# Toeplitz matrices copied on GpSimd into channel-major order, one block of 24 channels ahead

## The chip, the cores and the metric

The kernel runs on one core of one Trainium2 chip. The metric is the device time of one execution in microseconds (us), the median over several runs; less is better. The engines are named as in the profile: PE is TensorE (PEld its weight loads), DVE is VectorE, ACT is ScalarE, POOL is GpSimd and SP is SyncE, which here only issues DMAs.

## The reference

Four residual layers act on an image batch of 8 x 56 x 56 x 192 in fp32: a gated Toeplitz mixer, shifted-window attention, a depthwise 3x3 convolution, and a selective scan in four directions. The change lies in the first. Cut to it:

```python
p = silu(x @ p_w.T + p_b); q = silu(x @ q_w.T + q_b); v = silu(x @ v_w.T + v_b)   # 576 channels
a1 = rpe_mlp(positions, t1...) * decay      # 112 x 576: one coefficient for each offset and channel
a2 = rpe_mlp(positions, t2...) * decay
qv = q * v
o1 = toeplitz(qv along w, a1)               # for each channel: a 56 x 56 Toeplitz matrix times qv
o2 = toeplitz(qv along h, a2)
x = x + (p * (o1 + o2)) @ o_w.T + o_b
```

So for each of 576 channels and each of two axes, a 56 x 56 matrix whose entry depends only on the difference of its indices multiplies all lines of the images along that axis.

## The kernel before

A short first part computes the coefficients of both axes and stores them in HBM as `ext[axis]`, 24 pieces of 112 offsets x 24 channels. The main part, the scan of all images, runs from about 3350 us to the end and is scheduled by hand. Between them stand `products` (it computes q times v for an image and stores it in HBM as `qv_d`) and `toeplitz` (it multiplies by the Toeplitz matrices and stores `o_d`). Both run first for images 0 to 3 alone. Then both run for images 4 to 7 beside the other layers of image 0: a loop takes a step of that front work and then, by an estimate of its cost, steps of `products` and `toeplitz`. Outside the main part the framework plans the order of the instructions on each queue; each queue then runs in order.

`toeplitz` loops over the two axes, in each over six slabs of 96 channels (`c0`), in each slab over four blocks of 24 channels (`c1`), in each block over six groups of four channels (`c2`).

- **Slab.** `x` (tile `tzx`, 112 x 112 x 96, 43 KB per partition) is loaded at line 261 by eight DMAs on SP, 588 KB each. A partition holds one position along the axis; two halves of the lines of an image lie in partitions 0 to 55 and 56 to 111. On the first axis a packet is 10752 bytes, on the second 384. There are three such buffers in the first use and two in the second. The results overwrite the slab in place, and eight DMAs on POOL store it at line 288.
- **Block.** `tm` (112 x 112 x 24) holds 24 Toeplitz matrices, each a block-diagonal pair of the same 56 x 56 matrix. It is made by the DMA itself: two DMAs on SP (line 270), one for each diagonal block, whose source lets row `p` start one offset later than row `p - 1`, so that every partition reads 56 x 24 consecutive numbers. The channel is therefore the innermost dimension. There are three such tiles, used in turn, cleared once by POOL memsets at line 249; the zero corners are never written again.
- **Group.** Each of four channels is one fp32 matmul at line 274, which the trace shows as two records. Its weights are `t[:, :, c2 + c]`, 112 numbers per partition with 96 bytes from one to the next. Its moving operand is `x[:, :, channel]`, 112 numbers with 384 bytes from one to the next. The four results share a PSUM bank, and one copy at line 280 (DVE and ACT in turn, DVE alone in the second use) brings them back into the slab.

`ps_tz` has eight PSUM banks in the first use and four in the second. Lines written 79 in the profile are the front work of image 0, recorded under a helper's line.

Of the kernel before, what the change touches and what calls it, by code (L numbers as in the profile page):

```python
# [15 lines left out]
F32 = mybir.dt.float32  # L16
# [9 lines left out]
CP = 96  # L26
D1 = 576
CH = 448
NCH = L // CH
TT = 112  # L30
# [4 lines left out]
TC = 24  # L35
# [49 lines left out]
def model(ctx: ExitStack, tc: tile.TileContext, a: dict, out: bass.AP):  # L85
    nc = tc.nc
# [16 lines left out]
    ext = [dram.tile([D1 // TC, TT, TC], F32, name=f"ext{i}") for i in range(2)]  # L103
# [45 lines left out]
    with tc.tile_pool(name="rpe", bufs=2) as rp, tc.tile_pool(name="rpe_ps", bufs=2, space=PSUM) as rps:  # L149
# [19 lines left out]
        for i in range(2):  # L169
# [19 lines left out]
            for c in range(6):  # L189
# [4 lines left out]
                out=ext[i].rearrange("n p c -> p n c"), in_=eT.rearrange("p k (n c) -> p (k n) c", c=TC)  # L194
# [44 lines left out]
    def toeplitz(images, beside):  # L239
        G = len(images) * (H // 2)  # L240
        with (
            tc.tile_pool(name="tz", bufs=2) as sp,
            tc.tile_pool(name="tz_t", bufs=1) as tp,
            tc.tile_pool(name="tz_ps", bufs=4 if beside else 8, space=PSUM) as ps,
        ):

            tm = [tp.tile([TT, TT, TC], F32, name=f"tm{i}") for i in range(3)]
            for t in tm:
                nc.gpsimd.memset(t, 0.0)
            n_t = 0  # L250
            for ax in range(2):
                along_h = "(h u w) c -> u h w c"
                along_w = "(u h w) c -> u w h c"
                stored = "(w u h) c -> u w h c"
                size = dict(h=H, u=2) if ax == 0 else dict(w=W, u=2)
                for c0 in range(D1 // CP):
                    x = sp.tile([TT, G, CP], F32, name="tzx", bufs=2 if beside else 3)
                    for n, b in enumerate(images):
                        v = qv_d[b][c0].rearrange(along_w if ax else along_h, **size)
                        for u in range(2):  # L260
                            nc.sync.dma_start(out=x[u * W : (u + 1) * W, n * 28 : (n + 1) * 28, :], in_=v[u])
                    for c1 in range(0, CP, TC):
                        t = tm[n_t % 3]
                        n_t += 1
                        e = ext[1 - ax][(c0 * CP + c1) // TC]

                        src = bass.AP(e.tensor, e.offset, [[TC, W], [1, W * TC]])
                        for u in range(2):
                            dst = t[u * W : (u + 1) * W, u * W : (u + 1) * W, :].rearrange("p i c -> p (i c)")
                            nc.sync.dma_start(out=dst, in_=src)  # L270
                        for c2 in range(0, TC, 4):
                            po = ps.tile([TT, 4, G], F32, name="ps_tz")
                            for c in range(4):
                                nc.tensor.matmul(  # L274
                                    po[:, c, :], t[:, :, c2 + c], x[:, :, c1 + c2 + c], start=True, stop=True
                                )
                            cs = slice(c1 + c2, c1 + c2 + 4)
                            copy = nc.vector.tensor_copy if (c2 // 4) % 2 or beside else nc.scalar.copy

                            copy(  # L280
                                x[:, :, cs].rearrange("p (b g) c -> p b g c", g=28)[:, :, ::-1, :],
                                po.rearrange("p c (b g) -> p b g c", g=28),
                            )
                            yield 1.0
                    for n, b in enumerate(images):
                        v = o_d[ax][b][c0].rearrange(stored if ax else along_h, **size)
                        for u in range(2):
                            nc.gpsimd.dma_start(out=v[1 - u], in_=x[u * W : (u + 1) * W, n * 28 : (n + 1) * 28, :])  # L288
# [3 lines left out]
    for stage in (products, toeplitz):  # L292
        for _ in stage(now, False):
            pass


    with (
# [51 lines left out]
        for i in range(WS):  # L349
            for u in range(2):  # L350
                for j in range(WS):
                    at = (i * 2 + u) * WS + j
                    nc.scalar.dma_start(
                        out=bias[at : at + 1, :, :, u, :],
                        in_=a["table"][:, WS - 1 - i : 2 * WS - 1 - i, WS - 1 - j : 2 * WS - 1 - j].unsqueeze(0),
# [792 lines left out]
        with tc.tile_pool(name="ps0", bufs=4 if later else 8, space=PSUM) as ps:  # L1148
            log = costs.setdefault("front", [])
            first, others, spent = front(0), (us for stage in (products, toeplitz) for us in stage(later, True)), 0.0  # L1150
            while log_of(first, log) is not None:
                spent += 0.55 * sum(cost for _, cost in log[-1])
                while later and spent > 0.0:
                    us = next(others, None)
                    if us is None:
                        break
                    spent -= us
            for _ in others if later else ():
                pass
        wp2 = own.enter_context(tc.tile_pool(name="w2", bufs=1))  # L1160
        sp = own.enter_context(tc.tile_pool(name="sc", bufs=2))
# [208 lines left out]
```

## Time and profile before

| what | value |
|---|---|
| median of 3 runs | 21839.35 us (21826.98 to 21850.64) |
| the profiled execution | 21800.17 us, of it 21798.4 us span |
| busy over the span | PE 84%, PEld 45%, DVE 73%, ACT 56%, POOL 69% |
| mean granted TensorE clock | 0.888 |
| first `toeplitz`, first axis | matmuls from 534.2 us; second axis ends at 1098.7 us |
| second `toeplitz` | matmuls from 2261 to 3346 us, beside the front work of image 0 |
| matmul records of line 274 | 4608, mean 403 ns each, overlapped; 1031.5 us busy together |
| weight loads of line 274 | 4608, mean 319 ns each, overlapped; 1028.0 us busy together |
| POOL while `toeplitz` runs | 192 DMA issues of 513 ns and 6 memsets of 2342 ns |

A group's row in the profile has its line, engine and operation, the tiles written and read, the shapes and the count; then the time that at least one of them was running, the mean time of one, and the idle time of the engine just before them with what ended it. Where records overlap, as matmuls and weight loads do, busy time divided by count is the pitch from one to the next, and the mean is longer than that. The stretches view gives, for chosen intervals of the span, the busy time and count of each engine, the granted clock, the busy share of the DMA engines and the bytes moved in a second.

### The profile page before, as it was taken

How to read it: one execution, taken by the hardware profiler on the slowest of the kernel's cores; microseconds unless marked ns; L12 is line 12 of the kernel's file. 1: busy time of each engine (PE TensorE's matmuls, PEld its weight loads, DVE VectorE, ACT ScalarE, POOL GpSimd, SP SyncE). 2: the span in 40 equal slices, each digit the busy share in tenths (PEclk: the TensorE clock that was granted, in tenths of full speed). 3: DMA queues.
4: the chain of work that ended last, by engine and by line, in shares of the span. 5: the costliest groups of instructions: out<-in, count | busy, mean ns of one | idle time of the engine just before them, and what ended most of it. 6: DMA issues, size and time to landing. Idle time of an engine off the chain costs nothing. (4 is left out here: it accounts for less than half of the span.)

```text
span 21798.4 us, 194536 instructions
## 1 busy us (share of the span) xinstructions
PE 18274.4 (84%) x58396; PEld 9706.4 (45%) x58396; DVE 15858.5 (73%) x12604; ACT 12098.2 (56%) x28153; POOL 15084.9 (69%) x9175
## 2 busy tenths in 40 slices
PE   7978977888888989888888889888988888887777
PEld 4845654444443434444444434443444444343333
DVE  2122117996799768986799769976898589976998
ACT  3126114655666466755666566746675566656555
POOL 0000006887789778977788768976898678877998
PEclk9588868999999989998999989998999899998888
DMA  3931575444544455445644455345544464445443
GB/s 86 245 98 49 170 196 169 126 135 159 187 143 135 136 184 170 129 129 171 184 133 136 154 184 150 123 150 170 169 129 140 156 185 132 135 155 175 134 138 116
DMA packets 2419572, 3249.82 MB, mean 149 GB/s; under 512 B 917598, under 2 KB 2361024, under 8 KB 2387554
## 3 DMA queue, kind: packets, MB, share of 16 engines
q1 hardware_dynamic: 2398292, 3121.12, 47.5%
q0 software_dynamic: 15520, 116.14, 1.4%
q8 instruction: 463, 7.59, 0.1%
q14 instruction: 593, 4.86, 0.1%
q10 hardware_dynamic: 4704, 0.12, 0.0%
HBM read 2661.35 MB, written 575.48 MB: 148 GB/s over the span
## 5 line engine op out<-in xcount | busy, mean ns | idle before, releaser
L1007 POOL TENSOR_TENSOR ring<-du,bm 128x896 f32<-128x896 f32 x5376 | 9447.8, 1771 | 1983.9 <-ACT ring L1014 1937.8
L1054 PE MATMUL ps_y<-hc,ident_sb 128*128 128x448 f32 x21504 | 9818.6, 591 | 590.2 <-POOL hc L1039 573.3
L1024 ACT ACTIVATE ps_a<-delta,A_logs_sb 128x449 f32<-128x449 f32 x10752 | 6858.4, 638 | 331.5 <-DVE ring L1033 68.7
L1054 PEld LDWEIGHTS ps_y<-hc,ident_sb 128*128 128x128 f32 x21504 | 4271.5, 207 | 4640.8 <-issue 3494.9
L1033 DVE TENSOR_TENSOR_SCAN ps_a<-ps_a,ring 128x898 f32<-128x898 f32 x2688 | 5429.0, 2020 | 1062.5 <-ACT ring L1014 555.0
L1033 DVE TENSOR_TENSOR_SCAN ring<-ps_a,ring 128x898 f32<-128x898 f32 x2688 | 5423.0, 2017 | 420.4 <-ACT state L1046 177.3
L1039 POOL TENSOR_TENSOR hc<-ring,cm 128x896 f32<-128x896 f32 x2688 | 4758.0, 1770 | 860.9 <-DVE ring L1033 349.3
L1039 DVE TENSOR_TENSOR hc<-ps_a,cm 128x896 f32<-128x896 f32 x2688 | 2935.0, 1092 | 974.5 <-PE ps_y L1054 753.3
L1046 ACT COPY state<-ps_a 128x2 f32<-128x2 f32 x2687 | 425.3, 158 | 3254.0 <-DVE hc L1039 3250.0
L280 DVE COPY tzx<-ps_tz 112x448 f32<-112x448 f32 x432 | 269.8, 625 | 1389.9 <-PE ps_tz L274 1175.0
L274 PE MATMUL ps_tz<-tzx,tm 112*112 112x112 f32 x4608 | 1031.5, 403 | 257.6 <-DMA tm<-ext 233.0
L288 POOL DMA_DIRECT2D o<-tzx x192 | 97.3, 513 | 1653.6 <-DVE tzx L280 1318.7
L274 PEld LDWEIGHTS ps_tz<-tzx,tm 112*112 112x112 f32 x4608 | 1028.0, 319 | 295.2 <-issue 288.7
L817 PE MATMUL ps_f<-slab 128*128 128x448 f32 x2646 | 1086.4, 546 | 69.9 <-DMA slab<-dg_d 62.1
L1046 ACT COPY state<-ring 128x2 f32<-128x2 f32 x2688 | 504.9, 188 | 791.3 <-DVE ring L1033 778.4
L647 PE MATMUL ps_f<-ident_sb,slab 98*98 98x98 f32 x1344 | 336.5, 326 | 619.6 <-ACT slab L640 619.6
L749 PE MATMUL ps_f<-slab 96*96 96x448 f32 x1764 | 725.1, 547 | 47.7 <-DVE slab L736 47.7
L817 PEld LDWEIGHTS ps_f<-slab 128*128 128x128 f32 x2646 | 506.8, 192 | 560.5 <-issue 485.0
L79 PE MATMUL ps_f<-slab 96*96 96x448 f32 (+6 forms) x2306 | 731.2, 497 | 10.2 <-DMA slab<-x 4.9
L990 POOL TENSOR_TENSOR du<-delta,xcd 128x448 f32<-128x448 f32 x672 | 658.6, 980 | 23.6 <-DMA xcd<-xc 23.6
L647 PEld LDWEIGHTS ps_f<-ident_sb,slab 98*98 98x98 f32 x1344 | 203.9, 158 | 1033.7 <-ACT slab L640 814.6
L227 PE MATMUL ps_qv<-wqv,xn 96*128 96x384 f32 (+1 forms) x1200 | 527.0, 522 | 128.2 <-DVE xn L146 67.5
(218 smaller groups left out, 17070.7 us busy)
## 6 DMA issues: line engine op xcount, KB each, us to landing
bm<-bc SPq DMA_DIRECT2D x1792, 448.0 KB
cm<-bc SPq DMA_DIRECT2D x1792, 448.0 KB
xcd<-xc SPq DMA_DIRECT2D x840, 224.0 KB
dl<-slab SPq DMA_DIRECT2D x224, 672.0 KB
delta<-dl SPq DMA_DIRECT2D x224, 672.0 KB
tzx<-qv SPq DMA_DIRECT2D x192, 588.0 KB
o<-tzx POOLq DMA_DIRECT2D x192, 588.0 KB, 13.7
slab<-x SPq DMA_DIRECT2D x224, 336.0 KB
```

Of the source, the lines that this page charges most:

```text
L79: return f(*args, **kw)
L274: nc.tensor.matmul(po[:, c, :], t[:, :, c2 + c], x[:, :, c1 + c2 + c], start=True, stop=True)
L647: nc.tensor.transpose(p[:PT_, e * PT_ : (e + 1) * PT_], S[:, 3 * g + e, :], ident[:PT_, :PT_])
L749: nc.tensor.matmul(p[:CP, :CH], dg[:, k, t, :], xp[:, u, k, dy : dy + 8, dx : dx + W], start=t == 0, stop=t == 8,)
L817: nc.tensor.matmul(p[:, :CH], dg[:, t, :], xp[:, 8 * j + dy : 8 * j + dy + 8, dx : dx + W], start=t == 0, stop=t == 8,)
L990: nc.gpsimd.tensor_mul(du[:, 0, :], deltas[i][:, d, 1 : CH + 1], xcs.pop((i, d)))
L1007: nc.gpsimd.tensor_mul(hs[:, :, tokens(i)[0]], dus[i, d].to_broadcast([128, NG, CH]), bms[i, k])
L1024: nc.scalar.activation(dA[:, n, :], deltas[i][:, d, at : at + CH + 1], AF.Exp, scale=negA[:, slot, d, c : c + 1])
L1033: nc.vector.tensor_tensor_scan(h, dA, hs, 0.0, ALU.mult, ALU.add)
L1039: (nc.gpsimd if on_pool(d, k) else nc.vector).tensor_mul(hc, h[:, :, tokens(i)[0]], cms[i, k])
L1046: nc.scalar.copy(states[i][:, d, NG * k : NG * k + NG], h[:, :, tokens(i)[2]])
L1054: nc.tensor.matmul(yps[i, d][:, :CH], ident, hcs[g][:, n, :], start=k + n == 0, stop=k + n == NP + NG - 2)
```

## The change

The three tiles that the DMAs fill are now called `rows`. A function `fetch(n)` issues the two DMAs of block `n` into one of them, takes a new tile `tms[n]` of 112 x 24 x 112 (two buffers in turn, 10.5 KB per partition each), and has POOL copy the block into it with the channel outermost: the copy reads the row in order and writes with 448 bytes from one element to the next. `fetch(0)` is called before the first slab; the loop over blocks calls `fetch` for the next block, over the ends of slabs and of the axis, before it takes its own. The matmul reads `t[:, c2 + c, :]`, 112 consecutive numbers per partition. Its moving operand, the evictions, the loads and stores of the slabs and the bytes moved stay as they are.

```diff
-            tm = [tp.tile([TT, TT, TC], F32, name=f"tm{i}") for i in range(3)]
-            for t in tm:
+            rows = [tp.tile([TT, TT, TC], F32, name=f"tr{i}") for i in range(3)]
+            for t in rows:
                 nc.gpsimd.memset(t, 0.0)
+            axes = (0, 1)
+            order = [(ax, n) for ax in axes for n in range(D1 // TC)]
+            tms = {}
+
+            def fetch(n):
+                if n >= len(order):
+                    return
+                ax, m = order[n]
+                e = ext[1 - ax][m]
+                tr = rows[n % 3]
+                src = bass.AP(e.tensor, e.offset, [[TC, W], [1, W * TC]])
+                for u in range(2):
+                    dst = tr[u * W : (u + 1) * W, u * W : (u + 1) * W, :].rearrange("p i c -> p (i c)")
+                    nc.sync.dma_start(out=dst, in_=src)
+                tms[n] = sp.tile([TT, TC, TT], F32, name="tm")
+                nc.gpsimd.tensor_copy(tms[n].rearrange("p c i -> p i c"), tr)
+
+            fetch(0)
             n_t = 0
-            for ax in range(2):
+            for ax in axes:
...
                     for c1 in range(0, CP, TC):
-                        t = tm[n_t % 3]
+                        fetch(n_t + 1)
+                        t = tms.pop(n_t)
                         n_t += 1
-                        e = ext[1 - ax][(c0 * CP + c1) // TC]
-                        src = bass.AP(e.tensor, e.offset, [[TC, W], [1, W * TC]])
-                        for u in range(2):
-                            dst = t[u * W : (u + 1) * W, u * W : (u + 1) * W, :].rearrange("p i c -> p (i c)")
-                            nc.sync.dma_start(out=dst, in_=src)
                         for c2 in range(0, TC, 4):
                             po = ps.tile([TT, 4, G], F32, name="ps_tz")
                             for c in range(4):
                                 nc.tensor.matmul(
-                                    po[:, c, :], t[:, :, c2 + c], x[:, :, c1 + c2 + c], start=True, stop=True
+                                    po[:, c, :], t[:, c2 + c, :], x[:, :, c1 + c2 + c], start=True, stop=True
                                 )
```

## The prediction

> **What bounds the kernel now.** I begin with the page's part 1, for the balance of the whole run.
>
> ```profile
> PE 18274.4 (84%) x58396; PEld 9706.4 (45%) x58396; DVE 15858.5 (73%) x12604; ACT 12098.2 (56%) x28153; POOL 15084.9 (69%) x9175
> ```
>
> An average of this kind covers stages with different limits, and the chain of waits is no help (every share in it is 0%). The edited function runs only before 3346 us, so I cut that part with the stretches view, for the `tm` tile alone, at the four uses of the function: four images along either axis alone (534 to 757, 757 to 1099 us), then four images beside other work (2261 to 2837, 2837 to 3346 us).
>
> ```profile
> core 0: us, PE busy (x) PEld busy (x) POOL busy (x), PEclk, DMA share, GB/s
> 534.00:757.00 223.00, 212.50 (x960) 211.56 (x960) 0.00 (x0) 0.50 0.81 253
> 757.00:1099.00 342.00, 297.92 (x1344) 296.27 (x1344) 0.00 (x0) 0.50 0.92 228
> 2261.00:2837.00 576.00, 262.70 (x1152) 264.17 (x1152) 0.00 (x0) 0.82 0.59 178
> 2837.00:3346.00 509.00, 258.12 (x1152) 255.79 (x1152) 0.00 (x0) 0.57 0.69 185
> ```
>
> Stage 1 is TensorE's: 212.5 of 223 us. In stage 2 a slab of 96 channels takes 50 us by the starts of its matmuls, only 42.6 of it on PE: the transfers set it. In stage 3 all PE work fills 500 of 576 us (same view without the tile). In stage 4 PE waits. Each fp32 matmul is two records (2304 calls, 4608 records). 212.50/960 is 221 ns a record, although stage 3 has nearly full clock and its 262.70/1152 is still 228 ns. So the clock does not set it; an operand does. The groups:
>
> ```profile
> L274 PE MATMUL ps_tz<-tzx,tm 112*112 112x112 f32 x4608 | 1031.5, 403 | 257.6 <-DMA tm<-ext 233.0
> L274 PEld LDWEIGHTS ps_tz<-tzx,tm 112*112 112x112 f32 x4608 | 1028.0, 319 | 295.2 <-issue 288.7
> L249 POOL MEMSET tm<- 112x2688 f32 x6 | 13.8, 2342 | 673.7 <-DMA qv<-qv 673.7
> L288 POOL DMA_DIRECT2D o<-tzx x192 | 97.3, 513 | 1653.6 <-DVE tzx L280 1318.7
> ```
>
> PEld is as full as PE (1028.0 against 1031.5): weight loads go end to end, 319 ns each, overlapped. The control is the transpose of 112x112 by the identity, with contiguous operands, in the lines of 1400 to 1500 us:
>
> ```profile
> L79 PE MATMUL ps_f<-ident_sb,slab 112*96 112x112 f32 x255 | 25.4, 259 | 0.0
> ```
>
> 25.4/255 = 100 ns a record, its loads 163 ns each. Yet **two** operands differ: here the moving `x[:, :, ch]` steps 384 B too, and the change leaves it. One place separates them: the first Toeplitz matmul behind another one at full clock, whose weights were ready early (tile view at 2503.02, then the PE timeline from 2502.6):
>
> ```profile
> L274 PE MATMUL ps_tz<-tzx,tm x1: 365/365/365, 2503.0 to 2503.0; 112*112 112x112 f32 x1
> ```
>
> ```profile
> 2502.28 0.91 PE L79 MATMUL ps_f<-slab 96*128 96x448 f32 x2
> 2503.03 0.36 PE L274 MATMUL ps_tz<-tzx,tm 112*112 112x112 f32 x1
> ```
>
> It ends at 3.39, the one before at 3.19: 200 ns, with no weight load to wait for, against 95 to 100 ns for the control in the same position; its 365 ns stands against 259. About 70 such places give 200 to 205. **So weights cost 220 ns a record and the moving operand about 200, just beneath.**
>
> **The Trainium skill.** "TensorE: Matmul & The Clock Gate", section "LDWEIGHTS", prices a load at columns/1.2, an estimated 93 ns for 112; 163 ns for 96 contiguous columns (with latency) fits, the 220 ns pitch here does not. "SBUF — State Buffer", section "Door 1", says why: lines of 16 bytes, and a penalty for each access that crosses to a new one. It names no engine; the 200 ns suggest that it holds for the moving side too. "Who interferes with whom" there has DVE block GpSimd with two SBUF inputs or in a two-port mode; these evictions read PSUM at 625 ns for 448 elements, so I charge nothing, though no POOL copy is shown beside them.
>
> **The change, part by part.**
>
> *Weights contiguous.* The load falls beneath the moving operand; the pitch goes from 220 to **200 ns** (bounds 187, at which the contiguous control's few records at half clock follow each other, and 220). 20 ns x 4608 = 92 us of PE. By stage:
> - Stage 1: five slabs of 192 records, 44.6 us each; 3.8 us less each, 19 us. The transfers need 0.81 x 223/5 = 36.1 us a slab, so 40.8 still fits.
> - Stage 2: the transfers' 50 us stay; only the last slab's matmuls count, 4 us.
> - Stage 3: 1152 x 20 = 23 us, times PE's share 500/576: 20 us.
> - Stage 4: slabs start 94 us apart, in a loop that the SP timeline and PE's show:
>
> ```profile
> 3086.04 1.21 SPq L888 DMA_DIRECT2D dl<-slab  x2
> 3087.30 35.38 SPq L261 DMA_DIRECT2D tzx<-qv  x7
> 3122.72 3.48 SPq L270 DMA_DIRECT2D tm<-ext  x2
> ...
> 3132.83 1.41 PE L274 MATMUL ps_tz<-tzx,tm 112*112 112x112 f32 x5 [21.41 <-DMA tm<-ext]
> ```
>
> The slab's load sits on SP behind a `dl` store that waits for ACT and, before it, for PE's other work; then PE waits 21.4 us for data. From PE's start at 3132.8 to the next such load at 3180.7, three of the slab's four blocks and other work run on PE; the rest of the loop is transfer. So three blocks lie on it: 3 x 48 x 20 ns = 2.9 us, five times, and 3.8 us at the last slab: 18 us.
>
> *Fetch one block ahead.* The first `tm` of a slab now stands ahead of the slab's load on SP. At 3132.8 the last packet of the slab had started at 3129.1 and the matrix came after; 0 to 2 us over six slabs, I take half: 6 us. SP's other waits change little: a fetch waited for PE three blocks back, now for a copy one block farther back on PE. Packets and bytes stay.
>
> *96 copies on POOL.* POOL is idle here but for stores and memsets. No row has a copy of 112x2688 with 448 B between the elements it writes. Low end: L249 writes as many in 2.34 us. High end: "GPSIMD Engine Reference", "Performance pitfalls", has 2.9 cycles an element for reads with a step over 8 bytes; applied to writes, at 1.2 GHz, an estimated 6.5 us. I take the two-input rate of line 1007 (1771 ns for 896): 2688 x 1.98 ns = **5.3 us**. A block will take PE 9.6 us, so inside a slab the copy is hidden even at 6.5. At a slab's end it is queued behind eight stores (8 x 0.51 = 4.1 us) that wait 1.1 us for the last eviction: 1.1 + 4.1 + 5.3 = 10.5 against 9.6 us, and TensorE, next in line for the second block, waits 0.9 us less any gap before the slab. Five slabs of stage 1: 5 us at most, charged whole; the other stages have wider gaps. Stores queued behind a copy move by up to 5.3 us; the next user of their buffer is a slab away.
>
> *Start.* Fetch 0 waits for a memset (2.34 us) and now stands ahead of the first slab load on SP: 2 us, twice, less the matrix behind it: 2 us.
>
> *`tms`* adds two buffers of 10.5 KB per partition; no time.
>
> Sum: 19 + 4 + 20 + 24 - 5 - 2 = **60 us**. The profiled execution took 21800.2 us (1.8 us over its span) and lies 39 us under the median of the runs, so 21740 for a like execution and **21779** for the median.
>
> **Rivals.** A change of 0.2% is 44 us, about what a measurement of this kernel tells from none.
>
> *A, not felt* (0.19). The moving operand needs the full 220, or the gain of stages 3 and 4 is taken back by SP's order and the slab loads. Then only stage 1 and the last slabs remain, 0 to 40 us: about 21820. For it: transfers at 0.92 in stage 2, the loop of stage 4. Against: the 200 ns.
>
> *B, more* (0.11). The 200 ns was an effect of the strided load beside it, and the moving operand keeps up. At half clock the pitch is 187, at full clock 100. Stage 1 falls to its transfers' 37 us a slab (38 us), stage 2 gives 6, stage 3 1152 x 120 ns x 0.87 = 120, stage 4 36 to 115: about 240 us, 21600. Against: 70 like places.
>
> *C, slower: POOL becomes the bound* (0.18). A slab needs four copies, eight stores and the eviction: 4X + 5.2 us. At X = 9.7 this is stage 1's 44.6. With the 40 us of the other stages set against it, the loss passes 44 us at X = 12.3 us (4.6 ns an element). At X = 13, twice the high end: stage 1 +76, stage 2 +43, less 40 at most, and some 15 to 50 more in stages 3 and 4: 80 to 130, about 21945. For it: no strided write by POOL is in this trace. Against: every elementwise POOL row costs about 2 ns or less an element.
>
> **How the numbers follow.** My forecast has 0.52; its own gain runs from 30 to 100 us (pitch 187 to 205, copy 2.3 to 6.5), 21740 to 21810, about four fifths of it over 44 us. Faster: 0.52 x 0.8 + B 0.11 = 0.53; same: 0.52 x 0.2 + A 0.19 = 0.29; slower: C, 0.18. Range: 21680 takes in the forecast with what lies between it and B; 21880 takes in A and the mild half of C. B and the worse half of C, 0.2 together, are left out.
>
> **What would show it.** Right: L274's loads near 176 ns, PEld well under PE, PE's pitch near 200 ns at either clock; a POOL COPY row of 96 near 5 us; stage 1 at 41 us a slab, stage 2 still 50. Wrong: a pitch of 100 to 187 (B), or still 220 (A); a copy over 9.7 us, with PE waiting for POOL on `tm` (C); slabs of stage 4 still 94 us apart would take 14 us from the sum.

## The result, and the profile after

The changed kernel takes 21763.8 us (median of 8 runs, 21751.9 to 21794.8) against 21834.1 us for the kernel before beside it (8 runs): a ratio of 0.9968 with a 95% interval of 0.9958 to 0.9978, so 70 us less (48 to 92). The forecast was 60 us less. A second set of runs gave 0.9972 (0.9964 to 0.9980). The profiled execution took 21766.7 us, of it 21764.9 us span.

The groups first, from the page after; columns as before.

```profile
L267 POOL COPY tm<-tr 112x2688 f32<-112x2688 f32 x96 | 460.4, 4799 | 1192.3 <-PE ps_tz L289 553.2
L289 PE MATMUL ps_tz<-tzx,tm 112*112 112x112 f32 x4608 | 907.1, 370 | 319.0 <-DMA tr<-ext 203.1
L289 PEld LDWEIGHTS ps_tz<-tzx,tm 112*112 112x112 f32 x4608 | 879.9, 205 | 370.6 <-issue 362.5
```

The 4608 matmul records keep PE busy for 907 us in place of 1031. One weight load has a median of 193 ns in place of 320 (the trace's tile view). The 96 copies take 4.80 us each. PEld is still nearly as full as PE, where the prediction had named "PEld well under PE" as a sign of being right. But now it follows PE instead of driving it: with a moving operand in consecutive numbers (`moving_run` below) the same loads keep up with matmuls that are 98 ns apart.

The stretches view for the `tm` tile, cut at the same times as before:

```profile
core 0: us, PE busy (x) PEld busy (x) POOL busy (x), PEclk, DMA share, GB/s
534.00:757.00 223.00, 210.07 (x1086) 207.77 (x1086) 105.39 (x22) 0.93 0.87 282
757.00:1099.00 342.00, 236.12 (x1220) 233.43 (x1219) 115.20 (x24) 0.82 0.88 215
2261.00:2837.00 576.00, 248.80 (x1232) 234.13 (x1232) 120.21 (x25) 0.89 0.62 185
2837.00:3346.00 509.00, 208.70 (x1056) 201.52 (x1056) 100.72 (x21) 0.70 0.70 191
```

In the first line 210.07/1086 is 193 ns a record (221 before), and 126 more records fit into the same time. They belong to the sixth slab of the first axis: the cut at 757 us lies behind its fifth, so that the row called stage 2 holds one slab of the first axis, before as after. From start to start of the matmuls the median pitch is 192 ns in all four stages. The granted clock of stage 1 is 0.93 and was 0.50.

The table follows from the starts of the matmuls in each trace. "First use" runs from the first matmul of images 0 to 3 to their last, "second use" the same for images 4 to 7; the rest is all that comes behind. Two profiles each of the kernels before and after are given.

| kernel | first use, us | second use, us | end of the second | rest |
|---|---|---|---|---|
| before | 564.5, 592.6 | 1085.1, 1085.3 | 3346.3, 3362.1 | 18452, 18472 |
| after | 549.5, 553.0 | 1058.6, 1065.3 | 3313.7, 3315.3 | 18451, 18486 |
| fetch_only | 684.9 | 1112.7 | 3488.8 | 18475 |
| copy_own_block | 569.2 | 1048.0 | 3321.2 | 18499 |
| copy_twice | 587.8 | 1087.0 | 3377.5 | 18467 |
| slab_ahead | 581.8 | 966.5 | 3244.1 | 18458 |
| slab_ahead_later | 548.4 | 968.2 | 3204.9 | 18494 |
| both_in_runs | 566.1 | 943.5 | 3208.8 | 18474 |
| both_slab_ahead_later | 559.8 | 945.3 | 3194.4 | 18489 |

The edited stages end 31 to 48 us earlier. The medians say 64 and 70 us (two sets). The rest differs from one profile to the next by up to 48 us whatever the kernel, so the profiles neither show nor exclude a gain behind the edited stages; what the medians show beyond the stages' 31 to 48 us is not located.

### The profile page after: what moved, and what is told of

Read it like the earlier page. It is cut to its first block, busy times and chain, and to the rows that moved or that the text cites. A ratio compares the mean times of both kernels' runs of the same rounds, so it can differ in the third digit from the quotient of the medians.

```text
span 21764.9 us, 194702 instructions
## 1 busy us (share of the span) xinstructions
PE 18115.7 (83%) x58396; PEld 9550.3 (44%) x58396; DVE 15869.3 (73%) x12604; ACT 12101.2 (56%) x28153; POOL 15553.3 (71%) x9271
## 5 line engine op out<-in xcount | busy, mean ns | idle before, releaser
L267 POOL COPY tm<-tr 112x2688 f32<-112x2688 f32 x96 | 460.4, 4799 | 1192.3 <-PE ps_tz L289 553.2
L289 PE MATMUL ps_tz<-tzx,tm 112*112 112x112 f32 x4608 | 907.1, 370 | 319.0 <-DMA tr<-ext 203.1
L289 PEld LDWEIGHTS ps_tz<-tzx,tm 112*112 112x112 f32 x4608 | 879.9, 205 | 370.6 <-issue 362.5
L832 PEld LDWEIGHTS ps_f<-slab 128*128 128x128 f32 x2646 | 508.5, 193 | 559.8 <-issue 486.4
```

The source lines that it names most:

```text
L289: nc.tensor.matmul(po[:, c, :], t[:, c2 + c, :], x[:, :, c1 + c2 + c], start=True, stop=True)
L832: nc.tensor.matmul(p[:, :CH], dg[:, t, :], xp[:, 8 * j + dy : 8 * j + dy + 8, dx : dx + W], start=t == 0, stop=t == 8,)
```

## The experiments

**Repeats of both kernels**, unchanged.

> The kernel before, unchanged, profiled a second time: the first profiled execution (21800 us) lies 34 us under the median of its eight runs, and the two traces differ by only 33 us where the medians differ by 70. If executions differ from one to the next after the Toeplitz stages, those end here at 3346 +- 5 us again and the rest takes 18452 to 18490 us. If the first profile had caught lucky Toeplitz stages, they end here at 3360 us or later.

> The changed kernel, profiled and timed again beside the others of this set. Theory: 65 +- 20 us below the kernel before; the Toeplitz stages end at 3314 +- 5 us, 32 us earlier than before, and the pitch of a matmul record is 192 ns. Rival, that the change also shortens what follows them: the part after 3314 us is 20 us or more shorter than that of the kernel before on the same chip.

The second profile of before ends its edited stages at 3362 us, as the second of the two expectations had it (3360 or later), and not at 3346 +- 5; the rest is 20 us longer as well. So the first profile of before was a short execution in both parts: its first use took 564.5 us, the second profile's 592.6. That difference stands in the five slab periods of the second axis (248 against 259 us) and in the slab ahead of them (50 against 71); stage 1 differs by 3 us. After: 3315.3 us and 192 ns as expected; its rest (18486 us) is not shorter than before's, so the rival has no support. The median is 21776.6 us against 21841.0.

**Fetch ahead without the copy.**

```diff
-                tms[n] = sp.tile([TT, TC, TT], F32, name="tm")
-                nc.gpsimd.tensor_copy(tms[n].rearrange("p c i -> p i c"), tr)
+                tms[n] = tr
...
-                                    po[:, c, :], t[:, c2 + c, :], x[:, :, c1 + c2 + c], start=True, stop=True
+                                    po[:, c, :], t[:, :, c2 + c], x[:, :, c1 + c2 + c], start=True, stop=True
```

> The DMAs of a matrix are issued one block ahead as in the changed kernel, but there is no copy: TensorE reads the weights from the fetched tile with 96 bytes between them, as before. Theory, that the weights' pitch makes the gain: pitch 220 ns, 0 to 15 us below the kernel before. Rival, that the order on the queues (matrix ahead of the slab) makes it: 40 us or more below.

Measured: 21967.1 us, ratio 1.0063 (1.0050 to 1.0075). The pitch stayed at 220 ns, but the kernel is 126 us slower, which neither theory had. The SP timeline of this kernel in stage 2, and PE's behind it, show why (start, duration, line, tiles, count, and in brackets the idle time before it):

```profile
856.10 0.32 SPq L280 DMA_DIRECT2D tzx<-qv  x1
865.40 0.74 SPq L265 DMA_DIRECT2D tr<-ext  x2
866.19 21.33 SPq L280 DMA_DIRECT2D tzx<-qv  x7
```

```profile
904.38 0.97 PE L288 MATMUL ps_tz<-tzx,tr 112*112 112x112 f32 x3 [17.88 <-DMA tzx<-qv]
```

The fetch at 865.40 is the next slab's first matrix. It reuses the tile that PE reads in the second block of the current slab, and this block ended at 865.2 us. Seven of the eight DMAs of the next slab are queued behind it. The load therefore starts 22 us after its predecessor slab began (843.9), where the kernel before starts it 13 us after (870.3 against 857.4), and PE waits 17.9 us. Stage 2 takes 60 to 69 us a slab. So here a fetch placed one block ahead is harmful by itself. With the copy it is not, in the first use: the copy frees the fetched tile before PE comes to the block, and the changed kernel starts such a load 9 to 10 us into the slab (851.8 against 842.1). The SP lines before and after:

```profile
870.28 24.95 SPq L261 DMA_DIRECT2D tzx<-qv  x8
```

```profile
851.84 32.43 SPq L281 DMA_DIRECT2D tzx<-qv  x8
```

**Copy without the lead.**

```diff
-            fetch(0)
             n_t = 0
...
-                        fetch(n_t + 1)
+                        fetch(n_t)
```

> GpSimd copies each matrix, but fetch and copy stand at the block's own place, behind the stores of the slab before. Theory, that the first copy of a slab waits for the last eviction and eight stores (1.1 + 4.1 us) and then takes 4.8: pitch 192 ns, but in stage 1 TensorE waits some 8 to 10 us at each slab (48 us a slab instead of 39), which costs 40 to 55 us against the changed kernel in stage 1 and less elsewhere; the whole is then within 30 us of the kernel before. Rival, that one block ahead is of no matter since the transfers set the pace anyway: within 10 us of the changed kernel.

Measured: 21796.2 us, ratio 0.9979 (0.9973 to 0.9986), 20 us over the changed kernel of the same set, though the two intervals overlap. The expected wait is there; PE's timeline in stage 1:

```profile
584.87 37.21 PE L288 MATMUL ps_tz<-tzx,tm 112*112 112x112 f32 x192 [10.10 <-POOL tm L267]
```

The first three slabs take 47.2 us, as forecast. The next two take 37.0 and 38.7, so stage 1 is 23 us longer than in the changed kernel and not 40 to 55. POOL's timeline shows why: there the plan put the first copy of the next slab ahead of the eight stores, where PE no longer waits for it:

```profile
707.38 4.82 POOL L267 COPY tm<-tr 112x2688 f32<-112x2688 f32 x1 [4.46 <-PE ps_tz L288]
717.69 4.03 POOL L302 DMA_DIRECT2D o<-tzx  x8 [5.49 <-DMA tzx<-qv]
```

The second use is 11 to 17 us *shorter* than in the changed kernel: three slabs of stage 4 take 89 us in place of 94 to 100. There no fetch stands ahead of a slab's load, and part of the load goes before the `dl` store again; that this is the cause is argued here and not shown; `slab_ahead` below supports it. So the lead of one block gains in the first use and loses part of that in the second; the total lies 45 us under before and not within 30 as I had written.

**One operand at a time.** The moving operand of the changed kernel in consecutive numbers:

```diff
-                                    po[:, c, :], t[:, c2 + c, :], x[:, :, c1 + c2 + c], start=True, stop=True
+                                    po[:, c, :], t[:, c2 + c, :], t[:, c2 + c, :], start=True, stop=True
```

> The changed kernel with a moving operand of consecutive numbers: each Toeplitz matmul takes its 112 numbers from the copied matrix in place of x, so the slabs' values leave the products. Theory, that the 384-byte steps of the moving operand set the 192 ns of the changed kernel: the pitch falls to 95 to 105 ns where the clock is full (187 where it is half). Rival, that 192 ns is something else (the copy's tile, a clock, an issue rate): it stays near 190 ns at full clock.

And the kernel before with only its weights stepping:

```diff
-                                    po[:, c, :], t[:, :, c2 + c], x[:, :, c1 + c2 + c], start=True, stop=True
+                                    po[:, c, :], t[:, :, c2 + c],
+                                    t.rearrange("p i c -> p (i c)")[:, (c2 + c) * G : (c2 + c + 1) * G],
+                                    start=True, stop=True
```

> The kernel before with a moving operand of consecutive numbers, taken from the matrix in place of x (so the slabs' values leave the products); the weights keep their 96-byte steps. Theory, that the weights alone set the 220 ns: the pitch stays at 220 ns. Rival, that the two strided operands together do (they share something): it falls well below 210 ns.

The stretches view of each in stage 1 (all tiles; columns PE, PEld, DVE, ACT, POOL where present, then clock, DMA share, GB/s), `moving_run` first:

```profile
540.00:733.00 193.00, 106.58 (x927) 104.59 (x926) 35.75 (x59) 29.90 (x58) 107.34 (x59) 0.77 0.89 299
```

```profile
534.00:757.00 223.00, 213.96 (x967) 212.84 (x967) 37.46 (x60) 32.45 (x61) 0.50 0.81 253
```

In the first, 106.58/927 is 115 ns, a mixture: in that trace some 3760 records at full clock have a median pitch of 98 ns, some 730 at half clock 187. In the second, 213.96/967 is 221 ns. So stepping weights alone give 220 ns, a stepping moving operand alone gives 192, and neither gives 98. In the changed kernel the pitch is 192 ns at full and at half clock alike (some 3840 and 660 records). Both rivals fall. The two steps do not add: with both operands stepping, before, the pitch is 220 ns as with the weights alone. In one run each, beside 21817.1 us for the kernel before, `moving_run` took 21623.7 us and `weights_step_moving_run` 21800.7; both leave the slabs' values out of the products. The first use of `moving_run` still ends at 1095 us, so PE's time is no longer what ends that part.

**The copy doubled.**

```diff
                 nc.gpsimd.tensor_copy(tms[n].rearrange("p c i -> p i c"), tr)
+                nc.gpsimd.tensor_copy(tms[n].rearrange("p c i -> p i c"), tr)
```

> The changed kernel with every copy of a matrix done twice, so 9.6 us a block on GpSimd in place of 4.8; TensorE's work is the same. Theory, that the copy is hidden up to the point where four copies, eight stores and the eviction fill a slab: 4 x 9.6 + 5.2 = 43.6 us a slab in stage 1 against 39, stage 2 unchanged at 51 on average, and in all 20 to 60 us slower than the changed kernel. Rival, that GpSimd's place in the queue has slack everywhere: within 10 us of it.

Measured: 21844.1 us, ratio to before 1.0007 (0.9998 to 1.0015). The gain is gone: with 9.6 us a block the copy is no longer covered. That is more than the 20 to 60 us that were forecast against the changed kernel: 57 to 67 us in the two uses by the profiles, 76 to 85 by the ratios. Stage 1 takes 48 us a slab behind its first, 4 more than forecast. The second use takes 22 to 28 us more; there PE waits 18 us for the copies. PE's timeline at a slab's second block, then POOL's:

```profile
644.54 5.70 PE L290 MATMUL ps_tz<-tzx,tm 112*112 112x112 f32 x28 [10.03 <-POOL tm L268]
```

```profile
627.05 3.53 POOL L304 DMA_DIRECT2D o<-tzx  x7 [0.26 <-issue]
630.58 9.34 POOL L267 COPY tm<-tr 112x2688 f32<-112x2688 f32 x2
639.78 9.34 POOL L268 COPY tm<-tr 112x2688 f32<-112x2688 f32 x2
```

The plan put the first copies of two blocks ahead of their second copies, so that this block waited for three copies behind the stores. The mechanism was right; the sum had left out this order.

**The slab's load ahead.** The next slab is loaded behind the fetch made in a slab's second block; `load` holds the eight DMAs that stood at the slab's start.

```diff
                         fetch(n_t + 1)
+                        if c1 == TC:
+                            load(*divmod(ax * (D1 // CP) + c0 + 1, D1 // CP))
```

> The changed kernel with the next slab's load moved up on SP, behind the fetch made in the second block of the slab, in place of behind the fetch made in the fourth. Theory, that in stages 2 and 4 the first matrix of a slab, which now stands ahead of the slab's load and waits for a copy, starts that load late: stage 2 falls from 51 to 47 to 50 us a slab and stage 4 from 96 to 80 to 92; 20 to 80 us below the changed kernel. Rival, that the transfers' rate and PE's other work set these stages: within 15 us of it.

Measured: 21703.7 us, ratio 0.9945 (0.9932 to 0.9957), 113 us under before. That is 43 to 49 us under the changed kernel, a size that was expected, but not in these places. The second use falls by 92 to 99 us: stage 4 to 82 us a slab as forecast, and stage 3, which I had not named, gives some 36 of it. Stage 2 goes the other way, to 56 us a slab. POOL's timeline there:

```profile
953.66 9.36 POOL L267 COPY tm<-tr 112x2688 f32<-112x2688 f32 x2 [27.78 <-DMA tr<-ext]
```

In stage 2, where the DMA engines are busy for 0.91 of the time, the matrix of the fourth block now stands behind the slab's load: POOL waits 27.8 us for it and PE for POOL. In the second use the load had waited on SP behind other work, and there the lead pays. Hence the same step for the second use alone (`c1 == TC and beside`):

> The next slab's load moved up as in the run before, but only in the second use; the first use is as in the changed kernel. Theory, that the move pays where the load waited behind other work on SP (stages 3 and 4) and costs where the transfers are full and the next blocks' matrices then stand behind the slab (stage 2): the first use ends near 1090 again in place of 1118, and the whole is 15 to 30 us below the kernel with the load moved up in both uses. Rival: within 10 us of that kernel.

Measured: 21699.2 us, ratio 0.9941 (0.9927 to 0.9954). The trace shows what was expected: the first use takes 548 us again, the second 968. In the medians, 113 and 127 us under before in their sets, the 15 to 30 us of the theory are not resolved from the rival's 10.

**Both operands in runs.** ScalarE copies 24 channels of the slab into `xb`, one block ahead within a slab; for room the second use has two fetched tiles.

```diff
...
+                    def in_runs(c1):
+                        xb = sp.tile([TT, TC, G], F32, name="xb")
+                        nc.scalar.copy(xb.rearrange("p c g -> p g c"), x[:, :, c1 : c1 + TC])
+                        return xb
...
-                                    po[:, c, :], t[:, c2 + c, :], x[:, :, c1 + c2 + c], start=True, stop=True
+                                    po[:, c, :], t[:, c2 + c, :], xb[:, c2 + c, :], start=True, stop=True
```

> The changed kernel with the moving operand in runs too, with the right values: ScalarE copies 24 channels of the slab into a tile with the channel outermost, one block ahead within a slab, and the matmul reads that; in the second use two fetched tiles stand in place of three, for room. Theory, that only the operands' steps held the pitch: 98 ns at full clock, 187 at half; stage 1 stays near 37 to 40 us a slab and stage 2 near 51 (transfers), stages 3 and 4 give 60 to 150 us together; 60 to 150 us below the changed kernel. Rival, that the added ScalarE copies (2.5 us, exposed at each slab's start) and SP's order take it back: within 25 us of it.

Measured: 21693.9 us, ratio 0.9937 (0.9925 to 0.9950), 133 us under before: 63 to 68 us more than the change brings in its own sets, at the low end of the theory. The pitch is 98 ns at full clock. The added copies cost twice what I had put; the tile view of `xb` (count, then min/median/max ns), and as a control a ScalarE instruction on as many numbers that lie in a row (from the changed kernel's lines):

```profile
L284 ACT COPY xb<-tzx x96: 4703/4914/5147, 537.2 to 3198.5; 112x2688 f32<-112x2688 f32 x96
```

```profile
L900 ACT ACTIVATE slab<-slab 128x2688 f32<-128x2688 f32 x98 | 239.6, 2445 | 1.1
```

The first use does not gain (566 us, 13 to 17 more than the changed kernel's; stage 2 takes 57 us a slab and not 51). Then both steps:

> Both steps together: moving operand in runs, and the slab's load moved up in the second use. Theory, that they take away different waits (matmul time, and the wait for the slab): their gains add to at least three quarters, 120 to 230 us below the changed kernel. Rival, that both shorten the same loop of stage 4 and the front work of image 0 is next: no more than 30 us better than the better of the two.

Measured: 21678.9 us, ratio 0.9931 (0.9918 to 0.9943), 148 us under before. It beats the kernels before and after by more than their intervals. But the theory falls. Over the change's own 64 to 70 us, the two steps brought 57 to 63 and 63 to 68 us alone and bring 78 to 84 together, 15 us more than the better of them: the gains overlap, as the rival said. With the short matmuls the second use takes 944 us, and 945 with the slab's load moved up besides, so there the second step adds nothing. What holds it at that was not tried.

## Why the prediction was right, and where its steps were not

*The pitch* (forecast 200 ns, measured 192). The mechanism is shown: `weights_step_moving_run` isolates the 220 ns of the weights, `moving_run` the 192 ns of the moving operand. The 200 ns had been read where a stepping weight load ran beside the matmul. In such places of a trace (the first Toeplitz matmul directly behind another matmul at full clock, 76 to 84 of them) the median is 204 ns before, 193 after, and 98 in `weights_step_moving_run`: a stepping load beside it makes a stepping moving operand some 11 ns slower, and one in consecutive numbers not at all. So PE saved 124 us in place of 92. A load's own time was forecast near 176 ns; it is 193 in the changed kernel, beside the stepping moving operand, and 178 in `moving_run`.

*Stage 1* (forecast 19 us over five slabs). By the starts of the slabs 38.8 us each in place of 44.6, 29 us over five (26 in the second pair of profiles). How much of it lasts depends on which profile of before is taken: the next slab takes 67 us from start to start after the change, and 50 or 71 in the two profiles of before, as PE then waits for the data of the second axis (30 us, against 8 and 28). Against the first profile 17 us are lost there again, against the second none.

*Stage 2* (forecast: its pace stays, 4 us at the last slab). The pace of the second axis is 50 to 52 us a slab in all four profiles, as forecast. Stages 1 and 2 together are 12 to 43 us shorter, depending on which profiles are paired.

*Stage 3* (forecast 20 us). It takes 556 and 554 us against 576 and 574: 20 us. The agreement is luck, for two errors cancel: the pitch fell by 28 ns and not 20, which by the working of the forecast would give 28 us, but only about six tenths of PE's saving arrived, not nine.

*Stage 4* (forecast 24 us with the matrix ahead of the slab; measured -2 to 9 by the pairing of the profiles). **This step failed.** Between its first and its last slabs the starts lie 94 to 100 us apart, against 92 to 94 before: the sign of being wrong that the prediction had named for it. What little was gained lies at the first and the last slabs. I had three blocks on the loop. The SP timeline after, then PE's:

```profile
3057.95 1.21 SPq L903 DMA_DIRECT2D dl<-slab  x2
3059.52 41.37 SPq L281 DMA_DIRECT2D tzx<-qv  x8
```

```profile
3012.07 21.83 PE L289 MATMUL ps_tz<-tzx,tm 112*112 112x112 f32 x112 [27.21 <-DMA tr<-ext]
...
3053.24 1.03 PE L79 MATMUL ps_f<-slab,w_dt_sb 12*128 12x448 f32 x4
3054.20 3.38 PE L289 MATMUL ps_tz<-tzx,tm 112*112 112x112 f32 x16
```

The `dl` store at 3058.0 us carries what follows from the front matmuls at 3053.2, and the slab's load waits behind it. By then all but 16 of the slab's 192 records have run: 176 x 192 ns = 33.8 us lie on the loop, in place of 144 x 220 = 31.7 before. And all eight DMAs of the load, not seven, wait. The framework had planned SP's and PE's order anew; the prediction had read the loop from the trace of before and kept it. `slab_ahead` takes that wait away, and the second use falls by over 90 us.

*Fetch one block ahead* (forecast 6 us gained, "SP's other waits change little"). Wrong as it stands: `fetch_only` loses 126 us by such a wait. In the changed kernel the copy's early release of the tile hides this, but not in the second use, where `copy_own_block` is 11 to 17 us shorter.

*The copy* (forecast 5.3 us, measured 4.80). The wait at a slab's end was charged with 5 us; in the whole run PE waits for a copy once, 1.0 us, and its weight loads twice, 1.8 us. Nothing had been charged for DVE beside the copies, and they show none: all 96 lie between 4.70 and 4.89 us, and DVE's evictions take 625 ns as before. *The start* (forecast 2 us): the first matmul starts at 538.9 us against 534.2 and 532.6, 5 to 6 us.

So the sum of 60 us met the measured 64 and 70 with a term too small (PE's saving) and a term that failed (stage 4), and the profiles place only 31 to 48 us of it. The direction and the mechanism were right; that the total came so near is in part luck. Rival B held that the moving operand keeps up: it does not, and the 98 and 187 ns that B expected came only when that operand lay in runs too, with 133 us in all and not 240. Rival A named the transfers and SP: roughly half of PE's 124 us did not arrive by the medians and more by the profiles, and stage 4 shows SP's part in it. Rival C had a copy of 9.7 us as the point where stage 1 alone is back at its time before (its own terms give 9.85), the other stages' 40 us still gained, and a loss of 44 us only at 12.3. Measured, the whole gain is gone at 9.6 already, by the order on POOL and by the second use.

## What to carry to other kernels

Where a stream of matmuls keeps one pitch at either clock, as here 220 and then 192 ns, look at the steps of *both* operands, and find a place where one of them is already loaded: this gives the second limit before the first is removed. A fetch moved one block ahead takes with it the wait for its buffer; ask which load is queued behind that wait, and let a copy or another buffer free it early. And moving a load up paid here where it had waited on its queue (stages 3 and 4), and cost time where the transfers were nearly full (stage 2, DMA share 0.95 in the changed kernel).

## What the runs showed of the hardware

- "SBUF — State Buffer", section "Door 1", in the Trainium skill speaks of a penalty for each access to a new line without a figure; the only engine it ties to steps in SBUF is GpSimd (the prediction read it as naming none). For fp32 on TensorE here: records with 112 moving numbers 384 bytes apart follow each other at 192 ns, consecutive ones at 98 at full clock; loads of 112 weights 96 bytes apart follow each other at 220 ns, consecutive ones keep up with the 98. When both step, the pitch is the larger of the two, not their sum. That the lines of the section are the cause is not shown: no run has other steps than these.
- Copies that change the order of 2688 numbers per partition take 4.80 us on GpSimd and 4.9 on ScalarE: 1.79 and 1.83 ns a number, almost the same on two different engines. The one on GpSimd reads in order and writes 448 bytes apart; the one on ScalarE reads 24 numbers at a time and writes 448 bytes apart. A ScalarE instruction on 2688 numbers in a row takes 2.45 us (0.91 ns a number).
- The granted clock in stage 1 rose from 0.50 to 0.93 when the pitch fell from 220 to 192 ns, and the pitch did not depend on it: it was 192 ns at both. With consecutive operands it did: 98 and 187 ns. In `weights_step_moving_run` (220 ns) the clock was 0.50 too, in `moving_run` (98 ns at full clock) 0.77. What sets the clock is not shown.
